# Expert weights, table pieces and block order in the first layers of a transformer kernel: homes for all eight early blocks, a table in six pieces, a single block at the end of both loops

## The chip, the cores and the metric

The kernel runs on one core of a Trainium2 chip. The metric is the device time of one execution in microseconds. All times below are in microseconds. The engines are called by the names that the profile gives them: PE is TensorE (matrix products), DVE is VectorE, ACT is ScalarE, POOL is GpSimd and SP is SyncE, which here only issues DMA transfers. Each engine runs its own queue of instructions in order; semaphores tie the queues together.

## What is computed

The reference is a stack of two macaron blocks on 2048 tokens of width 128 (8 sequences of 256). The part that matters here is the mixture of experts, which is computed twice, before and after an attention:

```python
def _L0_ffn_ref(s, W_in, in_norm_w, Wr, expert_bias, Wg, Wu, Wd, enorm_w, out_norm_w, W_out):
    x = s.reshape(B * T, -1)
    h = rmsnorm(x @ W_in.T, in_norm_w)
    logits = h @ Wr.T
    _, idx = jax.lax.top_k(logits + expert_bias, TOP_K)      # 2 of 8 experts
    sel = jnp.take_along_axis(logits, idx, axis=-1)
    g_topk = jax.nn.softmax(sel, axis=-1)
    gates = jnp.zeros_like(logits).at[jnp.arange(N)[:, None], idx].set(g_topk)
    out = jnp.zeros_like(h)
    for e in range(Wg.shape[0]):
        gate = jax.nn.silu(h @ Wg[e].T)                      # 128 -> 512
        up = h @ Wu[e].T                                     # 128 -> 512
        oe = rmsnorm(gate * up @ Wd[e].T, enorm_w[e])        # 512 -> 128
        out = out + gates[:, e:e + 1] * oe
    s_hat = rmsnorm(out, out_norm_w) @ W_out.T
...
x = x + 0.5 * _L0_ffn_ref(_layernorm(x), ...)     # first layer of experts
x = x + _L0_attn_ref(_layernorm(x), ...)
x = x + 0.5 * _L0_ffn_ref(_layernorm(x), ...)     # second layer of experts
x = x + 0.5 * _L1_ffn_ref(...); x = x + _L1_attn_ref(...); x = x + 0.5 * _L1_ffn_ref(...)
```

## The kernel before

**Blocks of rows.** Each token goes to two experts. The kernel scatters a copy of every token's row into a region of its expert in DRAM (`hs`, line 470), reads the regions back in blocks, computes an expert on a block, and scatters the results to `y` in DRAM (line 769), from where the combination of the two results reads them (line 829). A row is 129 floats, 516 bytes.

There are two kinds of blocks. *Early blocks* (numbers 24 to 31 in tile names, called early block 0 to 7 here, one for each expert) are the first 128 rows of an expert; they can be read before all tokens are dispatched, at places known beforehand. *Table blocks* are the rest: numbers 0 to 14 are *pairs* (256 rows), numbers 15 to 23 are *singles* (128 rows). Which expert and which rows a table block has is found at run time, in a table that VectorE computes from the counts (`table`, line 564, in seven steps: counted, summed, paired, spared, singled, named, bounded). "Named" (lines 634 to 643) writes the tile `tab`: the expert of each block (line 634) and its first row (line 639). "Bounded" (lines 648 to 656) writes `far`, which sends rows beyond an expert's count to nowhere; it is first read when the result rows of table block 0 are addressed.

**The loop.** `work` (line 782) runs over the eight early blocks and then over the table blocks in the order of `TURNS[f]`, where f is the layer (0 or 1); blocks in `MORE` run only where the counts need them. For turn i it issues, in this order:

- gate: 4 products `pg` of the block's turned rows with the gate weights (line 722, in float32 each is two passes, so the profile counts 8), then SiLU on ScalarE (line 731)
- turn_rows of the *next* block: `pht`, a transposition of its rows (line 709), scaled by ScalarE for early blocks (line 712) and by VectorE for table blocks (line 714)
- up: 4 products `pu` (line 722), then the gated product `hg` on VectorE (line 738)
- `pieces[i]`, other work hung into turn i (the steps of the table, later a filter)
- down of the *previous* block: products `py` (line 745), squares on ScalarE (line 762), which also write the sums into column 128 of the result rows, the row product on VectorE (line 763, called so here; it reads `py` and the last columns of the weights), addresses (lines 766 and 767) and the scatter by POOL (line 769, one for each 128 rows). `py` has one bank, so the next down product waits for the row product of this one.
- fetches for block i + 3 on SP's queue: its rows, then its weights (`fetch_rows` and `fetch_weights`). For a table block each of these loads a number from `tab` into a register and then issues a DMA.

The weights of an expert are one piece of 832 KB (gate, up, down and norm, `WALL` columns). The pool tag `w` has four buffers; a load waits until the last reader of its buffer is done, which is the row product. Result rows of table blocks (`yrow`) have two buffers: before the squares of a block may be written, the scatters of the block two before it must have landed.

**Early blocks in the first layer.** `first_experts` (line 903) gives the weights of early blocks 0 to 2 places in the attention's idle tiles (`homes`); those of 3 to 7 take pool buffers, and seven of the eight loads are issued at the start of the kernel (line 910). The eighth, of early block 7, is issued in the loop, by the fetch of turn 4, when early block 3 has given its buffer back; table block 0 then takes the buffer of early block 4. The early blocks' rows are in tile `v0`, their result rows in `v1`; the table's scratch is behind the rows in `v0`. In the second layer (`second_lead`) the weights of early blocks 0 to 5 have such places, only 6 and 7 take pool buffers, and two are free.

**The table in the loop.** `run_experts` (line 891), for both layers:

```python
tab, far, steps = table(f, pc, gp, lead, scratch)
steps[0]()
steps = [*steps[1:5], both(*steps[5:7])]
steps += [lambda: None] * (E - len(steps))
experts(f, tab, far, y2s[f], lead["pool"], steps + pieces, lead)
```

So turns 0 to 3 carry one step each, turn 4 carries named and bounded together, and `pieces` (filter, constants for the attention, the clearing of the attention's tiles by POOL) begin at turn 8.

**After the loop** all engines meet at a branch (line 804); SP's reads of `y` wait until all scatters have landed and POOL has passed this on.

Of the kernel before, what the change touches and what calls it, by code (L numbers as in the profile page):

```python
# [22 lines left out]
E, DFF = 8, 512  # L23
# [9 lines left out]
ROW = D + 1  # L33
# [12 lines left out]
LEAD = 6, 8  # L46
LEADING = list(range(NT, NT + E))
TURNS = (
    [0, 1, 2, 15, 3, 4, 5, 16, 6, 7, 8, 17, 9, 10, 18, 11],
    [0, 1, 2, 15, 3, 4, 5, 6, 16, 7, 8, 9, 17, 10, 11, 12],  # L50
)
MORE = [12, 13, 14, 19, 20, 21, 22, 23], [13, 14, 18, 19, 20, 21, 22, 23]
REGION = NTOK + TT
# [5 lines left out]
WALL = 3 * DFF + D  # L59
# [14 lines left out]
def macaron_kernel(ctx: ExitStack, tc: tile.TileContext, a: dict, out: bass.AP):  # L74
# [110 lines left out]
    def both(*pieces):  # L185
        def run():
            for piece in pieces:
                piece()

        return run  # L190
# [488 lines left out]
    def experts(f, tab, far, y2, mp, pieces, lead):  # L679
# [17 lines left out]
        def fetch_rows(t):  # L697
            n, m = f"f{f}_{t}", blocks(t)
            if t in hst:
                return  # L700
            row = nc.values_load(tab[0:1, 0, t : t + 1], engines=[SP], min_val=1, max_val=HS_ROWS - TT)
            hst[t] = mp.tile([P, 2, ROW], F32, tag="hst", name=f"hst_{n}", bufs=4)[:, 0:m]
            nc.sync.dma_start(hst[t], hss[f][bass.ds(row, m * P), :].rearrange("(s p) c -> p s c", p=P))
# [78 lines left out]
        def work(turns, pieces):  # L782
            n = len(turns)
            for t in turns[:3]:
                fetch_weights(t)
                fetch_rows(t)
            turn_rows(turns[0])
            for i, t in enumerate(turns):
                sg = gate(t)
                if i + 1 < n:  # L790
                    turn_rows(turns[i + 1])
                up(t, sg)
                if i < len(pieces):
                    pieces[i]()
                if i > 0:
                    down(turns[i - 1])
                if i + 3 < n:
                    fetch_rows(turns[i + 3])
                    fetch_weights(turns[i + 3])
            down(turns[-1])  # L800

        work(LEADING + TURNS[f], pieces)
# [88 lines left out]
    def run_experts(f, pc, gp, lead, scratch, pieces):  # L891
        tab, far, steps = table(f, pc, gp, lead, scratch)
        steps[0]()
        steps = [*steps[1:5], both(*steps[5:7])]
        steps += [lambda: None] * (E - len(steps))
        experts(f, tab, far, y2s[f], lead["pool"], steps + pieces, lead)
        return weigh_up(f, gp)

    def wide_rows(t, n, o=0):

        return [t[:, o + i * ROW : o + i * ROW + ROW] for i in range(n)]

    def first_experts(parts, gp, pieces, qks, vs):

        with tc.tile_pool(name="moe0", bufs=2, reuse_waits="tile") as mp:
            homes = {0: qks[1][:, 0:WALL], 1: qks[1][:, WALL : 2 * WALL]}
            homes[2] = qks[0][:, 16 * ROW : 16 * ROW + WALL]
            lead = leading(0, gp, homes, wide_rows(vs[0], E), wide_rows(vs[1], E))
            lead["pool"] = mp
            for e in range(7):  # L910
                lead["weights"](e)
            found = {}

            def counted():
                found["pc"] = counts(0)
                zeros(found["pc"], gp)

            i, m = divmod(LEAD[0], TPC)
            parts[i][-2] = both(parts[i][-2], lead["flagged"])
            rows = parts[i][-1]  # L920
            parts[i][-1] = both(partial(rows, range(m)), lead["read"], partial(rows, range(m, TPC)))
            decays = decay_pieces()
            parts[-1][4] = both(parts[-1][4], decays[0])
            parts[-1][-1] = both(counted, parts[-1][-1])
            stagger(parts, 4)
            gates = run_experts(0, found["pc"], gp, lead, vs[0][:, E * ROW :], pieces)
        return gates, decays[1:]

    def second_lead(gp, qks, vs, ms):
# [658 lines left out]
    with tc.manual_schedule(engines={EN.PE, EN.DVE, EN.Activation, EN.SP}):  # L1588
        with tc.tile_pool(name="rows0", bufs=2) as gp:
            with tc.tile_pool(name="heads", bufs=1, reuse_waits="tile") as hp:  # L1590
                constant_pieces, attention, (*qks, v0, v1, m0, m1) = heads(hp)
                fold_in()
                parts = [[*dispatch(0, i, EARLY, gp)] for i in range(len(EARLY))]
                early = filter_pieces()
                idle = [fold_out, fold_mu, *constant_pieces()]
                idle += [lambda: None] * (len(early) - len(idle))
                pieces = [both(*two) for two in zip(early, idle)]
                gates, decays = first_experts(parts, gp, pieces, qks, (v0, v1))
                mixed = combined(0, gates, y2s[0], gp)
                lead = second_lead(gp, qks, (v0, v1), (m0, m1))  # L1600
                attention(mixed, [dispatch(1, i, LATE, gp) for i in range(len(LATE))], decays, lead)
                gates = second_experts(gp, lead, qks[1][:, 2 * WALL :])
            banks.close()
            tail(gates, y2s[1])
# [137 lines left out]
```

## Time and profile before

| what | us |
|---|---|
| median of 6 runs (lowest, highest) | 591.17 (588.67, 592.87) |
| the profiled execution, its own time | 591.93 |
| its span in the profile | 590.1 |
| TensorE busy in the span | 516.4 (88%) |
| first layer: first gate of the early blocks, first scatter of a table block, last scatter | 41.74, 83.80, 158.91 |
| second layer: the same | 370.22, 408.08, 481.37 |
| loads of weights in the loops, issue to landing, median | 4.7 |

How to read it. The page of the profile gives busy times of each engine and the chain of work that ended last, followed back from the end. The timeline gives instructions in order of time: start, length, engine, line, operation, what it writes and reads, and in brackets how long the engine sat idle before and what released it. The lengths of matrix products are modelled; their starts are measured, and the distance of starts is the better measure. SPq is SP's queue; a line there is the issue of a DMA, not its run. The table of stretches gives, for each from:to, its length, the busy time of PE, weight loads, DVE, ACT and POOL with the number of instructions, the share of the full clock that TensorE was granted, the busy share of the DMA engines and GB/s.

### The profile page before, as it was taken

Reading aid. Unit: us, or ns where it says so; the run is one execution under the profiler, and the core shown is the slowest. Engines: PE = TensorE matmul, PEld = TensorE weight load, DVE = VectorE, ACT = ScalarE, POOL = GpSimd, SP = SyncE. Lnnn points to the kernel's source line nnn. Section 1 sums busy time; section 2 is a strip of 40 time slices with the busy share of each in tenths; the row PEclk is TensorE's granted clock in tenths of the full one; section 3 lists DMA queues with packets and bytes.
Section 4 is the critical chain, followed back from the end, with each engine's and each line's share of the span. In section 5 each row is a group of like instructions: output and inputs, shape, how many; then the busy total and the mean of one; then the engine's idle time right before and its main releaser. Section 6 shows DMA issues by size and latency. Waiting matters only on the chain.

```text
span 590.1 us, 11358 instructions
## 1 busy us (share of the span) xinstructions
PE 516.4 (88%) x3954; PEld 401.8 (68%) x3954; DVE 357.3 (61%) x1129; ACT 277.7 (47%) x683; POOL 194.0 (33%) x202
## 2 busy tenths in 40 slices
PE   5459799999789989998898896989999978789996
PEld 5349798898645555565455553989999945468884
DVE  5776454564335766767767876664344324668775
ACT  4563232223334556557656654433232315884375
POOL 0677445753331201011002356532342335410100
PEclk9559899999989999999999999899999988989999
DMA  8833757666040355064063017455777515000002
GB/s 313 365 91 123 238 196 214 179 203 212 25 109 27 47 141 220 1 181 181 8 126 124 28 33 241 166 173 196 221 219 219 155 35 132 1 1 1 1 0 72
DMA packets 37952, 76.96 MB, mean 130 GB/s; under 512 B 4667, under 2 KB 27106, under 8 KB 36608
## 3 DMA queue, kind: packets, MB, share of 16 engines
q1 hardware_dynamic: 33360, 66.62, 37.0%
q0 software_dynamic: 4528, 9.52, 4.5%
q8 instruction: 35, 0.57, 0.4%
q14 instruction: 29, 0.24, 0.1%
HBM read 55.28 MB, written 21.44 MB: 130 GB/s over the span
## 4 chain that ended last, share of the span: by engine, by line
PE 63%; ACT 11%; DVE 11%; DMA 11%; issue 3%; SPq 1%; POOL 1%; DVEq 0%; ACTq 0%; POOLq 0%
PE pg_f L722 10%; PE pu_f L722 10%; PE py_f L745 8%; PE ps L1127 8%; DMA y<-yrow_f,idx_f 5%; ACT es L1164 4%; PE po L1174 3%; PE pvf L1496 2%; PE pgo L1523 2%; DMA hs<-blank 2%; DMA qk<-heads 2%; PE pin_f L374 1%; PE pm L1110 1%; DVE m L1147 1%; PE pht_f L709 1%
## 5 line engine op out<-in xcount | busy, mean ns | idle before, releaser
L1164 ACT ACTIVATE es<-ps 128x1024 f32<-128x1024 f32 x64 | 65.3, 1021 | 53.0 <-PE ps L1127 31.3
L1147 DVE TENSOR_REDUCE m<-pm 128x4 f32<-128x1024 f32 x64 | 77.4, 1220 | 12.9 <-PE pm L1110 12.8
L1127 PE MATMUL ps<-qa,qk 32*128 32x256 f32 x512 | 73.1, 401 | 11.8 <-ACT es L1164 9.5
L769 POOL DMA_INDIRECT y<-yrow_f,idx_f x57 | 56.1, 983 | 79.9 <-issue 44.0
L470 POOL DMA_INDIRECT hs<-hrow,posi_f x64 | 61.7, 964 | 53.9 <-issue 19.6
L738 DVE TENSOR_TENSOR hg_f<-pu_f,sg_f 128x1024 f32<-128x1024 f32 (+1 forms) x48 | 46.5, 969 | 50.1 <-PE pu_f L722 50.0
L1110 PE MATMUL pm<-qk 32*128 32x256 f32 x512 | 73.8, 400 | 0.9 <-ACT qk L1057 0.6
L762 ACT ACTIVATE ysq_f<-py_f 128x128 f32<-128x128 f32 x73 | 19.7, 274 | 102.2 <-PE py_f L745 90.6
L1127 PEld LDWEIGHTS ps<-qa,qk 32*128 32x128 f32 x512 | 43.5, 184 | 29.7 <-ACT es L1164 22.1
L731 ACT ACTIVATE sg_f<-pg_f 128x1024 f32<-128x1024 f32 (+1 forms) x48 | 39.3, 819 | 45.7 <-PE pg_f L722 45.7
L745 PE MATMUL py_f<-w_f,hg_f 128*128 128x128 f32 x456 | 56.7, 276 | 2.0 <-DVE idx_f L766 1.2
L745 PEld LDWEIGHTS py_f<-w_f,hg_f 128*128 128x128 f32 x456 | 54.9, 192 | 3.6 <-DVE yrow_f L763 2.3
L722 PE MATMUL pg_f<-ht_f,w_f 128*128 128x256 f32 (+1 forms) x256 | 54.8, 357 | 0.1
L722 PE MATMUL pu_f<-ht_f,w_f 128*128 128x256 f32 (+1 forms) x256 | 54.7, 357 | 0.0
L1110 PEld LDWEIGHTS pm<-qk 32*128 32x128 f32 x512 | 44.5, 184 | 3.4 <-issue 1.5
L722 PEld LDWEIGHTS pu_f<-ht_f,w_f 128*128 128x128 f32 x256 | 43.0, 191 | 4.5
L722 PEld LDWEIGHTS pg_f<-ht_f,w_f 128*128 128x128 f32 x256 | 42.9, 191 | 4.3 <-issue 0.3
L171 POOL TENSOR_TENSOR cf_f<-cf_f,mhalf 128x8 f32<-128x8 f32 (+1 forms) x9 | 13.5, 1502 | 65.6 <-DVE cf_f L834 64.2
L763 DVE TENSOR_TENSOR yrow_f<-py_f,w_f 128x256 f32<-128x256 f32 (+1 forms) x32 | 12.7, 396 | 35.7 <-ACT ysq_f L762 33.1
L1174 PE MATMUL po<-es,v 128*32 128x256 f32 x512 | 34.3, 385 | 0.0
L1159 DVE TENSOR_TENSOR qa<-pmt,qk 128x256 f32<-128x256 f32 x32 | 13.5, 422 | 25.7 <-PE pmt L1153 25.6
L714 DVE TENSOR_SCALAR ht_f<-pht_f,pack 128x256 f32<-128x256 f32 (+1 forms) x32 | 14.5, 453 | 17.8 <-PE pht_f L709 17.8
(327 smaller groups left out, 990.0 us busy)
## 6 DMA issues: line engine op xcount, KB each, us to landing
w_f<-in_wall_dram SPq DMA_DIRECT2D x32, 832.0 KB, 4.7
hs<-blank SPq DMA_DIRECT2D x8, 1032.0 KB, 15.7
qk<-in_wall_dram SPq DMA_DIRECT2D x7, 832.0 KB, 5.2
w_lead<-in_wall_dram SPq DMA_DIRECT2D x7, 832.0 KB, 5.7
y_f<-y SPq DMA_DIRECT2D x14, 258.0 KB, 3.4
hst_f<-hs SPq DMA_DIRECT2D x25, 129.0 KB
pack<-in_pack_dram SPq DMA_DIRECT2D x1, 1729.0 KB, 8.6
v<-in_wall_dram SPq DMA_DIRECT2D x2, 832.0 KB
```

What stands on the lines that cost most here:

```text
L470: ins = nc.gpsimd.indirect_dma_start(out=hss[f], out_offset=bass.IndirectOffsetOnAxis(ap=st["posi"][:, t, k : k + 1], axis=0), in_=hrow[:, ...
L722: nc.tensor.matmul(ph[:, k, :], w[t][:, o + k * P : o + k * P + P], ht[t], start=True, stop=True)
L731: nc.scalar.activation(sg, pg, AF.Silu)
L738: nc.vector.tensor_mul(hg[t], pu, sg)
L745: nc.tensor.matmul(py[:, s, :], hg[t][:, k, ts(s, P)], w[t][:, 2 * DFF + k * D : 2 * DFF + k * D + D], start=(k == 0), stop=(k == NFC - 1),)
L762: nc.scalar.activation(sq[:, s], py[:, s], AF.Square, accum_out=yrow[:, s, D : D + 1])
L769: ins = nc.gpsimd.indirect_dma_start(out=y2, out_offset=bass.IndirectOffsetOnAxis(ap=idx[:, s : s + 1], axis=0), in_=yrow[:, s, :], in_off ...
L1110: nc.tensor.matmul(sc[:, jj, i, :], qs[c][r, g, col + i * P : col + (i + 1) * P], ks[c][r, g, col : col + S], start=True, stop=True,)
L1127: nc.tensor.matmul(sc[:, jj, i, :], ks[c][r, g, col + i * P : col + (i + 1) * P], tops[s][r, :], start=True, stop=True,)
L1147: nc.vector.tensor_reduce(m, sc, AX.X, ALU.max, negate=True)
L1164: nc.scalar.activation(es, sc, AF.Exp, scale=scale)
L1174: nc.tensor.matmul(po[32 * j : 32 * j + 32, :], vs[c][:, (b % 2) * 2 + i, (g % 2) * (H // 2) + (g // 2) * 4 + j, :], ess[s, j // 2][:, j % ...
```

## The change

Four edits, in the first layer's early blocks and in the loop that both layers share:

1. The weights of early block 3 get a place in `v1`, so that the pool's four buffers take early blocks 4 to 7, and all eight loads are issued at the start. The early blocks' result rows move from `v1` to `m0` (seven of them) and behind the early rows in `v0` (the eighth). The table's scratch moves from `v0` to `m1`.
2. The table's steps named and bounded are separate pieces: turn 4 carries named, turn 5 carries bounded. This holds for both layers.
3. For the first table block alone (the fetch of turn 5), in both layers, the weights are fetched ahead of the rows on SP's queue.
4. The order of table blocks: in layer 0 single 18 stands behind pair 11, not ahead of it; in layer 1 single 17 stands at the end, behind pair 12, not between pairs 9 and 10. The set of blocks is the same.

```diff
@@ -46,8 +46,8 @@
 TURNS = (
-    [0, 1, 2, 15, 3, 4, 5, 16, 6, 7, 8, 17, 9, 10, 18, 11],
-    [0, 1, 2, 15, 3, 4, 5, 6, 16, 7, 8, 9, 17, 10, 11, 12],
+    [0, 1, 2, 15, 3, 4, 5, 16, 6, 7, 8, 17, 9, 10, 11, 18],
+    [0, 1, 2, 15, 3, 4, 5, 6, 16, 7, 8, 9, 10, 11, 12, 17],
 )
@@ -795,8 +795,10 @@
                 if i + 3 < n:
-                    fetch_rows(turns[i + 3])
-                    fetch_weights(turns[i + 3])
+
+                    first = turns[i + 3] == TURNS[f][0]
+                    for fetch in (fetch_weights, fetch_rows) if first else (fetch_rows, fetch_weights):
+                        fetch(turns[i + 3])
             down(turns[-1])
@@ -891,8 +893,7 @@
         steps[0]()
-        steps = [*steps[1:5], both(*steps[5:7])]
-        steps += [lambda: None] * (E - len(steps))
+        steps = steps[1:] + [lambda: None] * (E + 1 - len(steps))
         experts(f, tab, far, y2s[f], lead["pool"], steps + pieces, lead)
@@ -900,14 +901,15 @@
-    def first_experts(parts, gp, pieces, qks, vs):
+    def first_experts(parts, gp, pieces, qks, vs, ms):
...
-            homes[2] = qks[0][:, 16 * ROW : 16 * ROW + WALL]
-            lead = leading(0, gp, homes, wide_rows(vs[0], E), wide_rows(vs[1], E))
+            homes[2], homes[3] = qks[0][:, 16 * ROW : 16 * ROW + WALL], vs[1][:, 0:WALL]
+            yrows = wide_rows(ms[0], 7) + wide_rows(vs[0], 1, E * ROW)
+            lead = leading(0, gp, homes, wide_rows(vs[0], E), yrows)
             lead["pool"] = mp
-            for e in range(7):
+            for e in range(E):
                 lead["weights"](e)
@@ -923,7 +925,7 @@
-            gates = run_experts(0, found["pc"], gp, lead, vs[0][:, E * ROW :], pieces)
+            gates = run_experts(0, found["pc"], gp, lead, ms[1], pieces)
@@ -1595,7 +1597,7 @@
-                gates, decays = first_experts(parts, gp, pieces, qks, (v0, v1))
+                gates, decays = first_experts(parts, gp, pieces, qks, (v0, v1), (m0, m1))
```

## The prediction

> **What bounds the kernel now.** I read the page first (span, busy shares, chain), then the chain of waits around both expert loops, then the timeline of the engines and of SyncE's queue there, and last the granted clock by stretch.
>
> ```profile
> span 590.1 us, 11358 instructions
> PE 516.4 (88%) x3954; PEld 401.8 (68%) x3954; DVE 357.3 (61%) x1129; ACT 277.7 (47%) x683; POOL 194.0 (33%) x202
> PE 63%; ACT 11%; DVE 11%; DMA 11%; issue 3%; SPq 1%; POOL 1%; DVEq 0%; ACTq 0%; POOLq 0%
> ```
>
> TensorE sets the time, so the change is worth the TensorE idle time that it removes. The chain in the first layer's early blocks (start, length, what):
>
> ```profile
> 59.07 0.28 DVE tab_room L648
> ...
> 60.56 0.23 DVE tab_far L656
> 60.79 0.16 DVE v L763
> ...
> 61.00 5.72 DMA w_lead<-in_wall_dram
> 66.72 0.14 issue
> 66.86 1.45 PE pg_f L722 x8
> ```
>
> The table's last piece runs on VectorE up to 60.79, delays the row product (L763) of early block 3, and only that frees the weight buffer for early block 7, whose load then takes 5.72. The timeline (start, length, engine; in brackets idle time and releaser) shows the stops and the ends of both loops:
>
> ```profile
> 60.99 1.16 PE L745 MATMUL py_f<-w_lead,hg_f 128*128 128x128 f32 x8 [1.53 <-DVE v L763]
> 62.23 0.38 SPq L703 DMA_DIRECT2D hst_f<-hs  x1
> 66.86 1.45 PE L722 MATMUL pg_f<-ht_f,w_lead 128*128 128x128 f32 x8 [1.92 <-DMA w_lead<-in_wall_dram]
> ...
> 153.45 2.05 PE L745 MATMUL py_f<-w_f,hg_f 128*128 128x128 f32 x16 [0.78 <-DVE yrow_f L763]
> 158.91 0.97 POOL L769 DMA_INDIRECT y<-yrow_f,idx_f  x1 [0.31 <-ACT gates L673]
> ...
> 387.81 0.40 SPq L703 DMA_DIRECT2D hst_f<-hs  x1
> 389.00 0.35 SPq L695 DMA_DIRECT2D w_f<-in_wall_dram  x1
> 389.08 1.16 PE L745 MATMUL py_f<-qk,hg_f 128*128 128x128 f32 x8 [1.51 <-DVE m L763]
> ...
> 475.89 2.05 PE L745 MATMUL py_f<-w_f,hg_f 128*128 128x128 f32 x16 [1.18 <-DVE idx_f L766]
> 481.37 0.98 POOL L769 DMA_INDIRECT y<-yrow_f,idx_f  x1 [0.30 <-DVE gates L676]
> ```
>
> Layer one stops twice (1.53 and 1.92), layer two once (1.51). The granted clock by stretch (from:to, length, busy times by engine, clock, DMA share, GB/s) shows what a stop costs afterwards:
>
> ```profile
> 67.50:71.00 3.50, 3.50 (x19) 3.50 (x18) 0.93 (x2) 0.60 (x1) 0.16 (x1) 0.51 1.00 385
> 367.90:371.30 3.40, 2.87 (x12) 2.57 (x13) 2.31 (x14) 1.49 (x2) 2.48 (x4) 0.50 1.00 410
> 371.30:374.70 3.40, 3.40 (x18) 3.40 (x18) 0.38 (x1) 1.02 (x3) 2.49 (x4) 0.50 0.86 335
> ```
>
> After the 1.92 stop TensorE ran at half clock for 3.4 us. At layer two's start the half clock lasted from the first matmul at 368.0 to 374.7, some 6.6 us.
>
> **The change part by part.**
>
> *Early weights and table, layer one.* Warm, eight single-block matmuls take 0.89, a transposition 0.11 (0.21 at half clock). With the table cut in two, the part "named" (57.39 to 59.07) still stands ahead of early block 3's row product, which then ends near 59.3, and block 4's down product starts at 59.33, not 60.99. TensorE goes on without a stop: gate of 6 at 60.25, up of 6 to 62.14, down of 5 at 62.18, gate of 7 at 63.07 (its weights have been there since about 30) to 63.96. The part "bounded" takes 1.72 (59.07 to 60.79). It follows the gated product (0.62) of early block 5 that starts at 59.62, so it runs 60.24 to 61.96, and early block 4's row product frees its weight buffer 0.17 later, at 62.13.
>
> Here the new wait begins. Table block 0 takes that buffer, and SyncE's queue now has its weights ahead of its rows: weights out at 62.17, rows 1.1 later (as 63.95 to 65.07). Today the rows went out at 62.23 and landed at 67.49 by the trace's landing events, 0.77 behind early block 7's weights, hidden under that block's gate. TensorE takes the transposition of these rows before early block 7's up product, so everything from 63.96 on queues behind it, on VectorE too (table block 0's scaling, L714, stands ahead of early block 7's gated product). A weight load took 4.36 (77.15 to 81.51) to 5.72 (61.00 to 66.72); the two nearest are 5.72 and 4.56 (72.47 to 77.03), and I take 5.1. Two-block rows landed 0.36 to 0.90 behind the weights ahead of them; I take 0.75. With 0.14 from landing to TensorE: 62.17 + 5.1 + 0.75 + 0.14 = 68.2 (bounds 67.0 and 68.9). So two stops of 1.53 and 1.92 become one of 4.2. What follows up to table block 0's gate is 2.0 warm (0.22 + 0.89 + 0.89), plus half of a slow spell of 3.4 to 6.6 (I take 5.0): 68.2 + 2.0 + 2.5 = 72.7. Today that gate starts at 71.46. So **+1.2** (bounds: 67.0 + 2.0 + 1.7 = 70.7, -0.7; 68.9 + 2.0 + 3.3 = 74.2, +2.8). The rows of table block 1 and its weights go out behind, at 64.4 and 65.5 (66.45 today), and are needed at about 74 and 77.
>
> [...]
>
> *The same in layer two.* Weight buffers are free there and the rows' copies have their places, so only the order matters. "Named" ends at 387.17; early block 3's row product follows at once, and block 4's down product starts at 387.45 against 389.08: 1.63 gained. In the built program SyncE's two table loads each wait for VectorE on their own, so the weights need only L634 (ends 385.66) and, with the 0.87 from table load to issue, leave at 386.57; the rows leave at about 387.8 as now. Weights land in 4.53 (389.00 to 393.53), rows 0.9 behind (394.43): 392.0, and TensorE can take them at 392.14, when it gets there (393.75 - 1.63 = 392.12). **-1.6**; if the load takes 5.72, only -0.4.
>
> *A single block last.* Rows used: a pair's down product to its first square 1.99 (472.77 to 474.76), to its row product 0.65, on to the next down product 0.48; row product to scatter 1.44, scatter to scatter 1.28; for a single 1.09, 0.40 and 1.30 (151.61, 152.70, 153.10, 154.40). Layer one: the last up product still ends at 151.61; the pair's square is at 153.60, row product 154.25, the single's down product 154.73, scatters 155.69 and 156.97; the single is ready at 157.52, but POOL is busy, so 158.25 against 158.91: **-0.66**. Layer two: before the last up product ends, a pair's down product (1.79) is done in place of the single's (0.89), so 472.77 + 0.89 = 473.66, then 475.65, 476.30, 476.78; scatters 477.74, 479.02, 480.30 against 481.37: **-1.07**. Landing and what follows start from the last scatter, so this reaches the end. Bounds: layer one 0 to -0.7, layer two -0.5 to -1.1.
>
> *The middle of layer two's loop* no longer has a single between blocks 9 and 10; the gate at 463.81 took 1.94 in the chain where others take 1.73, its weights being late: **-0.2** (0 to -0.35).
>
> *Costed at nothing.* The eighth early load at the start: 832 KB; by the packets in the trace each early load moves in 2.0 us and the last ends at 28.1, so 30.2; SyncE next needs it at 34.44, for the twelfth scatter, issued at 31.9. Without that 1.7 of cover each us late would move the early rows. The early blocks' rows in other tiles: the same instructions; POOL's clearing of the first v tile (86.09) now also waits for early block 7's scatter (landed by 83.00): 3 us of cover, and behind it stands only the next scatter.
>
> Sum: +1.2 - 1.6 - 0.66 - 1.07 - 0.2 = **-2.3**. Against the profiled execution's own 591.93 (span 590.1) that is 589.6; it stood 0.76 above the median of the runs, so for the median 591.17 - 2.3 = **588.8**.
>
> **The rivals.** (1) Layer one's rows come early and the clock returns at once: term -0.7, sum -4.2, **587.0**. For: loads of 4.36 to 4.56 in quiet stretches. Against: at 62 to 68 early blocks' scatters share the engines, and the loads there took 5.72 and more. (2) That term at its dear end: +2.8, sum -0.7, **590.4**, no change that can be told. For: the 6.6 spell. (3) Slower: row buffers. Each loop's closing single must wait, before its squares, for the scatters of the pair two blocks back, which has the same of two buffers. Those are issued at 153.40 and 475.45 (as above, one block earlier), and the squares are due at 155.82 and 477.87. POOL's queue leaves 0.73 of slack, so a landing of up to 3.15 is free, and every us beyond costs one at each end. For: beside weight loads a scatter took 5.2 to 5.8 (458.87 to 464.04; 63.63 to 69.46). Against: at the ends no weights move (last issues 140.15 and 461.69), and scatters land in 2.2 to 3.2. At 5.5: -2.3 + 2 x 2.35 = +2.4, **593.6**; it turns slower from a landing of 4.3.
>
> **How the numbers follow.** Under 0.3% (1.8 us) this kernel can't be told from itself. Chances: forecast 0.50, rival one 0.17, two 0.17, three 0.16. The forecast's own range, from its bounds less their corners, is 587.4 to 590.6; about 0.7 of it lies below 589.4. So faster 0.17 + 0.35 = 0.52; same 0.15 + 0.17 = 0.32; slower 0.16. The range takes in rivals one and two and leaves out most of three: 586.8 to 591.8.
>
> **What would show it.** Right: no TensorE wait on early block 7's weights; the stop at 60.99 gone, a wait of 3 to 5 us ahead of the transposition of table block 0's rows with the DMA of hs as releaser, and a half-clock spell behind it; in layer two no stop at 389; last scatters 0.7 and 1.1 sooner against the last up product. Wrong: a table block 0 gate before 70.7 or after 74.2; squares of the closing singles waiting for a scatter; a new stop in layer two over 1 us.

## The result, and the profile after

| | before | after |
|---|---|---|
| median of the runs shown (lowest, highest) | 590.37 of 46 (586.74, 593.42) | 593.78 of 20 (591.30, 596.79) |
| the profiled execution, its own time | 591.93 | 593.28 |
| its span | 590.1 | 591.5 |

The ratio is 1.0065 with a 95% interval of 1.0049 to 1.0081. The change is 3.4 us slower. The forecast was 588.8, 2.3 us faster, with a range of 586.8 to 591.8.

The page of the changed kernel (span, busy time of TensorE, shares of the chain that ended last):

```profile
span 591.5 us, 11348 instructions
...
PE 516.9 (87%) x3954; PEld 401.8 (68%) x3954; DVE 357.6 (60%) x1129; ACT 277.6 (47%) x683; POOL 194.6 (33%) x202
...
PE 44%; ACT 10%; DMA 8%; DVE 7%; issue 2%; POOL 0%; SPq 0%; ACTq 0%; DVEq 0%; POOLq 0%
```

TensorE runs the same 3954 products and is busy 0.5 us longer, so of the 1.4 us between these two spans some 0.9 is idle time. The shares of the chain, 44% here and 63% before, can't be compared: they add up to 71% here, since the chain of the changed kernel is followed back only to 160.14 us, before to 1.45. The timeline of layer one's early blocks (start, length, engine, line, operation; in brackets idle time and releaser):

```profile
61.43 0.33 SPq L695 DMA_DIRECT2D w_f<-in_wall_dram  x1
61.46 1.06 PE L745 MATMUL py_f<-w_lead,hg_f 128*128 128x128 f32 x8
...
63.06 1.63 SPq L703 DMA_DIRECT2D hst_f<-hs  x2
...
67.46 0.69 PE L709 MATMUL pht_f<-ident,hst_f 128*128 128x128 f32 x2 [4.05 <-DMA hst_f<-hs]
...
71.35 2.79 PE L722 MATMUL pg_f<-ht_f,w_f 128*128 128x256 f32 x8
```

Both old stops are gone. One of 4.05 us, for the rows of table block 0, stands in their place. In the table of stretches (from:to, length, busy times of PE, weight loads, DVE, ACT, POOL, then clock, DMA share, GB/s) two spells of half clock of some 6.8 us each show (the expectations call such a spell two windows). One begins 1.2 us before this stop ends, the other stands behind the first loop:

```profile
66.30:73.20 6.90, 5.74 (x23) 5.38 (x24) 1.69 (x5) 0.37 (x2) 0.71 (x1) 0.51 0.63 181
158.50:165.30 6.80, 5.17 (x14) 3.56 (x15) 1.34 (x6) 1.12 (x4) 1.21 (x2) 0.50 0.08 24
```

The timeline at the end of the first loop:

```profile
155.54 1.16 PE L745 MATMUL py_f<-w_f,hg_f 128*128 128x128 f32 x8 [1.18 <-DVE yrow_f L763]
...
159.04 0.97 POOL L769 DMA_INDIRECT y<-yrow_f,idx_f  x1 [0.30 <-DVEq L806]
...
160.13 3.32 PE L197 MATMUL warm_f<-pack,ident 128*128 128x512 f32 x4 [3.43 <-ACT dec L283]
...
163.24 2.94 PE L290 MATMUL ptf<-filt,pack 128*128 128x128 f32 x16
...
164.89 2.99 SPq L831 DMA_DIRECT2D y_f<-y  x6
```

The fetch of y (`y_f`) leaves 5.85 us after the start of the last scatter. Before, these were 158.91 and 163.15, 4.24 apart:

```profile
163.15 2.98 SPq L829 DMA_DIRECT2D y_f<-y  x6
```

And layer two, its early blocks and its end:

```profile
388.70 0.35 SPq L695 DMA_DIRECT2D w_f<-in_wall_dram  x1
...
390.10 1.57 SPq L703 DMA_DIRECT2D hst_f<-hs  x2
...
395.45 0.44 PE L709 MATMUL pht_f<-ident,hst_f 128*128 128x128 f32 x2 [0.86 <-DMA hst_f<-hs]
...
397.52 1.89 PE L722 MATMUL pg_f<-ht_f,w_f 128*128 128x256 f32 x8
...
482.17 0.98 POOL L769 DMA_INDIRECT y<-yrow_f,idx_f  x1 [0.30 <-ACT gates L673]
...
487.00 4.81 SPq L831 DMA_DIRECT2D y_f<-y  x8
```

Here too the stop (1.51) is gone, a smaller one (0.86) has come, and from the last scatter to the fetch of y it is 4.83, before 3.39 (481.37 to 484.76).

The single execution that the profile shows tells of 1.35 us; the medians of 3.4. To see what is typical, the same distances were read from the trace of every kernel below that ran on a chip like this one. For each layer: first gate to the gate of table block 1 (block 1, since a slow spell can run into block 0's gate, as the one to 73.2 does here), from there to the last scatter, from there to the fetch of y.

| kernel | L1 early | L1 loop and tail | L1 landing | L2 early | L2 loop and tail | L2 landing |
|---|---|---|---|---|---|---|
| before | 34.29 | 82.88 | 4.24 | 30.11 | 81.04 | 3.40 |
| after | 35.59 | 82.23 | 5.84 | 29.54 | 80.08 | 4.83 |
| order_l0 | 32.42 | 82.22 | 6.24 | 30.29 | 81.19 | 3.40 |
| order_l1 | 33.53 | 82.88 | 4.25 | 29.74 | 79.45 | 4.93 |
| early_only | 36.29 | 82.91 | 4.24 | 29.25 | 80.53 | 3.65 |
| early_rows_first | 33.05 | 82.89 | 4.40 | 28.39 | 80.50 | 3.41 |
| after_warm | 37.56 | 82.23 | 5.69 | 29.46 | 79.46 | 4.96 |
| four_orders | 31.74 | 82.22 | 6.16 | 28.05 | 79.46 | 4.71 |
| late_branch | 30.90 | 82.22 | 4.82 | 28.71 | 79.44 | 3.69 |
| home_four_2 | 32.87 | 82.87 | 4.24 | 28.92 | 80.97 | 3.39 |

The three kernels with the old early code (before, order_l0, order_l1) have 32.42 to 34.29 in the first column, mean 33.41: the profiled execution of before was the dearest of them. The granted clock goes with this. From the first gate to block 1's it was at half for 8.7 us in before, 2.6 in order_l0 and 4.3 in order_l1 (11.5 in after, 11.6 in early_only). The spell behind the 1.92 stop of before is missing in order_l0, though its stop at the same place is longer (timeline, then stretch; the clock is the third number from the end):

```profile
65.52 1.13 PE L722 MATMUL pg_f<-ht_f,w_lead 128*128 128x128 f32 x8 [2.06 <-DMA w_lead<-in_wall_dram]
65.50:69.00 3.50, 3.13 (x26) 2.96 (x26) 1.17 (x2) 0.91 (x3) 1.17 (x2) 1.00 1.04 381
```

### The profile page after: what moved, and what is told of

It is laid out like the page before. It is cut to its first block, busy times and chain, and to the rows that moved or that the text cites. A ratio compares the mean times of both kernels' runs of the same rounds, so it can differ in the third digit from the quotient of the medians.

```text
span 591.5 us, 11348 instructions
## 1 busy us (share of the span) xinstructions
PE 516.9 (87%) x3954; PEld 401.8 (68%) x3954; DVE 357.6 (60%) x1129; ACT 277.6 (47%) x683; POOL 194.6 (33%) x202
## 4 chain that ended last, share of the span: by engine, by line
PE 44%; ACT 10%; DMA 8%; DVE 7%; issue 2%; POOL 0%; SPq 0%; ACTq 0%; DVEq 0%; POOLq 0%
PE ps L1129 8%; PE pg_f L722 5%; PE pu_f L722 5%; PE py_f L745 4%; ACT es L1166 4%; PE po L1176 3%; DMA qk<-heads 3%; DMA y<-yrow_f,idx_f 3%; PE pvf L1498 2%; PE pgo L1525 2%; PE pm L1112 2%; DVE m L1149 2%; PE pk_m L1442 1%; ACT xn_m L1407 1%; DMA w_f<-in_wall_dram 1%
```

## The experiments

The kernel before was timed beside each group of kernels. It took 590 us on two chips and 620 us on three; a ratio holds for its own chip.

| kernel | before on that chip | this | ratio, 95% interval |
|---|---|---|---|
| order_l0 | 589.70 | 590.56 | 1.0013 (0.9996 to 1.0030) |
| order_l1 | 589.70 | 590.89 | 1.0027 (1.0011 to 1.0044) |
| early_only | 589.70 | 593.05 | 1.0054 (1.0033 to 1.0075) |
| early_rows_first | 589.70 | 587.22 | 0.9944 (0.9919 to 0.9969) |
| after_rows_first | 619.73 | 616.10 | 0.9955 (0.9929 to 0.9980) |
| rows_first_fill | 619.73 | 617.19 | 0.9938 (0.9913 to 0.9962) |
| home_four | 619.73 | 614.43 | 0.9917 (0.9888 to 0.9946) |
| after_warm | 590.36 | 590.84 | 1.0009 (0.9980 to 1.0038) |
| four_orders | 590.36 | 587.57 | 0.9949 (0.9925 to 0.9973) |
| late_branch | 590.36 | 587.99 | 0.9969 (0.9946 to 0.9991) |
| home_four_2 | 590.36 | 587.34 | 0.9963 (0.9937 to 0.9988) |
| home_four_weights | 620.55 | 615.42 | 0.9916 (0.9885 to 0.9946) |
| after_home | 620.55 | 617.52 | 0.9959 (0.9936 to 0.9983) |
| home_four_weights_2 | 620.25 | 615.73 | 0.9931 (0.9906 to 0.9955) |
| after_home_2 | 620.25 | 618.90 | 0.9969 (0.9949 to 0.9989) |
| after_again | 620.87 | 621.87 | 1.0004 (0.9981 to 1.0026) |
| after_home_3 | 620.87 | 616.83 | 0.9926 (0.9897 to 0.9956) |
| home_four_weights_3 | 620.87 | 615.39 | 0.9914 (0.9883 to 0.9945) |

### The parts alone

order_l0 and order_l1 change one row of `TURNS` in the kernel before:

```diff
-    [0, 1, 2, 15, 3, 4, 5, 16, 6, 7, 8, 17, 9, 10, 18, 11],
+    [0, 1, 2, 15, 3, 4, 5, 16, 6, 7, 8, 17, 9, 10, 11, 18],
```

> The kernel before with the first layer's order of the changed kernel alone (single 18 behind pair 11). Theory A (the loss sits in the early blocks, where table block 0's rows leave behind its weights): the order alone gives the forecast's 0.66 us, ratio 0.999. Theory B (a single at the end of the first loop lets TensorE stop around 150 to 160, and the clock is halved in the filter and the warm-up products that stand ahead of the attention): 1.5 to 2.5 us slower, ratio 1.003 to 1.004, with a half-clock spell of 6.8 us at about 158 to 165 in the trace and the transposition of the combined rows behind the warm-up products.

> The kernel before with the second layer's order alone (single 17 last). Theory A and B both: the forecast's 1.07 + 0.2 = 1.3 us faster, ratio 0.998. A third theory (C: the order itself costs, since with pairs 9 and 10 next to one another the loads of weights come due closer together): 0.5 to 1 us slower, ratio 1.001 to 1.002, with longer waits for weights between blocks 8 and 11.

early_only is the changed kernel with both rows put back. early_rows_first takes edit 3 out of that as well:

```diff
-                    first = turns[i + 3] == TURNS[f][0]
-                    for fetch in (fetch_weights, fetch_rows) if first else (fetch_rows, fetch_weights):
-                        fetch(turns[i + 3])
+                    fetch_rows(turns[i + 3])
+                    fetch_weights(turns[i + 3])
```

> The changed kernel with both orders of blocks as before: homes for all early weights, the table in six pieces and weights ahead of rows remain. Theory A: most of the loss of 3.4 us is here, ratio 1.004 to 1.006, with the 4 us wait ahead of the transposition of table block 0's rows and two windows at half clock in layer one. By the trace of the changed kernel alone +1.3 in layer one and -0.6 in layer two make +0.7, ratio 1.001. Theory B: 1.001 or less, since the loss comes from the orders.

> As early_only, but rows ahead of weights for every block, as before. Theory A: table block 0's rows leave at about 60.5 us and land by 63.5, so early block 7's up and down products go on and TensorE stops only once, for 1 to 2 us, for the weights ahead of block 0's gate, at about 67.5 in place of 71.5; layer two gains 1 to 2 us. Together 3 to 5 us faster than the kernel before, ratio 0.992 to 0.995. Theory B: the order of these two loads matters little, since the weights bound the start of table block 0 anyway: ratio 0.999 to 1.001.

Neither theory has it all, though theory A has the early part. That part costs 3.2 us (0.0054 x 590), and taking edit 3 out of it turns that into a gain of 3.3 (0.0056 x 590). So homes and table in six pieces are worth 0.6%, and the order of two loads costs 1.1%. Each new order, which the forecast had faster, came out slower: by 1.6 us in layer two, and by 0.8 in layer one, where the interval still includes no change. order_l0's trace has the spell of half clock behind the loop that theory B named (156.8 to 163.6). order_l1's median fits theory C, but its trace does not: from block 1's gate to the fetch of y it took 84.38 against 84.44 before. That execution was the fastest of its twelve (589.67; the median is 590.89), so what the median shows beyond it is open.

The timeline of early_rows_first, to be read beside that of the changed kernel:

```profile
60.63 0.38 SPq L703 DMA_DIRECT2D hst_f<-hs  x1
...
62.38 0.35 SPq L695 DMA_DIRECT2D w_f<-in_wall_dram  x1
...
63.25 0.44 PE L709 MATMUL pht_f<-ident,hst_f 128*128 128x128 f32 x2 [0.48 <-DMA hst_f<-hs]
...
68.41 3.50 PE L722 MATMUL pg_f<-ht_f,w_f 128*128 128x256 f32 x8 [2.94 <-DMA w_f<-in_wall_dram]
```

The rows leave 2.4 us sooner, the weights only 0.95 later. TensorE goes on with early block 7 and stops 2.94 for the weights, where the changed kernel stopped 4.05 for the rows and had the transposition, early block 7's up product and a down product still to do behind it.

after_rows_first takes edit 3 out of the changed kernel itself:

> The changed kernel with rows ahead of weights for every block, as before; homes, table in six pieces and both new orders remain. If the order of these two loads is the main loss, and the parts add up (0.9944 without the new orders, 1.0013 and 1.0027 for the orders alone), ratio 0.998, some 6 us (0.010) under the changed kernel. If instead the new orders only cost something beside a late start of the loop, ratio 0.993 to 0.995.

0.9955, with an interval that reaches from the one expectation to the edge of the other. It ran on a chip of the 620 us kind, of which more at the end.

### Why weights ahead of rows lose

SyncE's queue, instruction by instruction, has a semaphore wait on VectorE in the changed kernel from 57.54 to 61.31, directly ahead of the issue of table block 0's weights at 61.43. The table had been ready for them at 57.5; what is waited for is early block 4's row product (61.00 to 61.28), which gives the buffer back. The rows stand behind. If that wait is the cause, edit 3 must lose nothing once the buffer is free. home_four gives early block 4's weights a home too (rows first, orders of before); home_four_weights puts the weights first in layer one on top of it; after_home adds the home to the changed kernel as it is:

```diff
+            homes[4] = vs[0][:, 0:WALL]
+            rows = wide_rows(ms[0], 7) + wide_rows(vs[0], 1, WALL)
-            yrows = wide_rows(ms[0], 7) + wide_rows(vs[0], 1, E * ROW)
-            lead = leading(0, gp, homes, wide_rows(vs[0], E), yrows)
+            yrows = wide_rows(ms[1], 7) + wide_rows(vs[0], 1, WALL + ROW)
+            lead = leading(0, gp, homes, rows, yrows)
...
-            gates = run_experts(0, found["pc"], gp, lead, ms[1], pieces)
+            gates = run_experts(0, found["pc"], gp, lead, qks[1][:, 2 * WALL :], pieces)
```

> early_rows_first (the order of blocks of before, rows ahead of weights) with a home for the weights of early block 4 as well (in the first v tile; the early rows move to the first m tile, the result rows to the second, the table's scratch behind the weights in the second qk tile), so that table block 0's load finds a free buffer. If the wait of 2.94 us ahead of block 0's gate stems from that buffer: weights leave 1.4 to 1.8 us sooner, the wait shrinks to 1.0 to 1.5 us, ratio 0.990 to 0.992 (0.9944 without it). If the loads only get in each other's way sooner: ratio 0.994 to 0.996, the wait moving to block 1.

> home_four again, on the chip of the two kernels above, to compare with them: ratio 0.989 to 0.993.

On the chip of the 590 us kind home_four brought no more than early_rows_first (0.9963 against 0.9944, intervals overlapping), and its trace says why: the weights still left at 62.35. They now stood behind the rows, which stood on the queue to 60.69 for the last dispatch scatter (landed at 60.67). So the free buffer was of no use there with the rows first, and the weights first need a free buffer.

> home_four (orders of before) with the weights of table block 0 ahead of its rows in layer one alone. In the changed kernel these weights were ready to leave at 57.5 us and stood 3.8 us on SyncE's queue for the buffer of early block 4, with the rows behind them; in home_four the rows stand on the queue until 60.7 for the last dispatch scatter and the weights leave at 62.4. Theory H (the order is good or bad only by who stands on the queue): with the buffer free the weights leave at about 57.6 and land by 63, the rows leave at 60.7 as before and land by 63.5; no stop over 1 us, no half-clock window, the gate of table block 1 comes 28.5 to 30 us after the first gate (32.9 in home_four, 34.3 before); ratio 0.985 to 0.990. Theory I (the load needs the DMA engines to itself; rows behind it land 4 us late wherever it starts): ratio 0.994 to 0.998.

> The changed kernel as it is, both orders and weights ahead of rows in both layers, with the one further home for early block 4's weights, so that nothing stands on SyncE's queue for a buffer. Theory H: the early loss goes and the early gain comes, 7 to 8 us under the changed kernel in layer one, ratio 0.991 to 0.995. Theory I: ratio 1.002 to 1.007.

> home_four_weights on another chip. On the chip of the last run the kernel before took 620 us, with VectorE and ScalarE standing still for some 12 us at the start of the early blocks, so table block 0's loads were not late there in any order and the two theories were not told apart. Theory H: the gate of table block 1 comes 28.5 to 30 us after the first gate, ratio 0.985 to 0.990; theory I: 33 to 35 us, ratio 0.994 to 0.998.

> after_home on another chip, for the same reason. Theory H: that gate 28.5 to 30 us after the first, ratio 0.989 to 0.995 where the changed kernel has 1.0065. Theory I: 34 to 36 us, ratio 1.002 to 1.007.

> The changed kernel itself, as the measure for after_home on one and the same chip: ratio 1.004 to 1.009 on a chip where the kernel before takes 590 us; on one where it takes 620 us both theories leave it open.

> after_home beside the changed kernel on one chip. Theory H (weights ahead of rows lose only by the buffer wait at the head of SyncE's queue): at least 0.008 under after_again where the kernel before takes 590 us, 0.003 or more where it takes 620. Theory I (weights ahead of rows are bad in themselves): within 0.003 of after_again.

> The best kernel so far on that chip too, with the orders of before: on a chip where the kernel before takes 590 us ratio 0.985 to 0.990 by theory H, 0.994 to 0.998 by theory I; where it takes 620 us 0.990 to 0.994 as in the two runs there.

All of these ran on chips of the 620 us kind, so the numbers expected for the other kind stay untried. after_home's first two ratios (0.9959 and 0.9969) lie between the ranges of both theories. The last three kernels share one chip. The timeline of after_again, which is the changed kernel:

```profile
84.46 0.33 SPq L695 DMA_DIRECT2D w_f<-in_wall_dram  x1
...
86.09 1.55 SPq L703 DMA_DIRECT2D hst_f<-hs  x2
...
89.95 0.44 PE L709 MATMUL pht_f<-ident,hst_f 128*128 128x128 f32 x2 [3.54 <-DMA hst_f<-hs]
...
93.57 1.97 PE L722 MATMUL pg_f<-ht_f,w_f 128*128 128x256 f32 x8
```

and of after_home_3, the same with the further home:

```profile
80.00 0.33 SPq L695 DMA_DIRECT2D w_f<-in_wall_dram  x1
...
81.75 1.56 SPq L703 DMA_DIRECT2D hst_f<-hs  x2
...
86.29 0.44 PE L709 MATMUL pht_f<-ident,hst_f 128*128 128x128 f32 x2 [0.42 <-DMA hst_f<-hs]
...
88.35 1.89 PE L722 MATMUL pg_f<-ht_f,w_f 128*128 128x256 f32 x8
```

The stop goes from 3.54 to 0.42, the gate of table block 0 comes 5.1 us sooner after the first gate (37.12 against 42.20), and the time falls from 621.87 to 616.83, by 5.0: 0.0078 in the ratio, where theory H asked for 0.003 and theory I for less. SyncE's wait for the buffer, 80.48 to 84.34 in after_again, is absent in after_home_3. Rows behind weights are harmless there once the buffer is free, and theory I falls. A gain from weights ahead of rows does not show: on the chip that ran both, home_four_weights (0.9916) lies level with home_four (0.9917).

### The clock behind the stop

after_warm fills the 4 us stop of the changed kernel with products that nobody reads:

```diff
                 if i + 1 < n:
+                    if f == 0 and turns[i + 1] == TURNS[f][0]:
+                        keep_warm(bank("warm_r", "sa"), 16)
                     turn_rows(turns[i + 1])
```

> The changed kernel with 3.7 us of idle products (eight passes, result unused) on TensorE between early block 7's gate and the transposition of table block 0's rows in layer one, so that TensorE works while it waits for these rows. Theory F (half of the early loss is the clock, halved for two windows behind the 4 us stop): no half-clock spell at 66 to 73, the gate of table block 1 comes 33 to 34 us after the first gate in place of 35.6, ratio 1.001 to 1.004 where the changed kernel has 1.0065. Theory G (the rows' landing alone decides): that gate stays at 35 to 36, ratio 1.005 to 1.007.

The median fell to 1.0009, as theory F wants. The profiled execution does not show it:

```profile
62.86 3.60 PE L197 MATMUL warm_r<-pack,ident 128*128 128x512 f32 x8
...
69.73 0.66 PE L709 MATMUL pht_f<-ident,hst_f 128*128 128x128 f32 x2 [3.27 <-DMA hst_f<-hs]
```

In that one the last sixteenth of the rows landed 6.9 us after their issue (62.70 to 69.59; 4.35 in the changed kernel), so TensorE stopped after all and the clock fell to half from 68.7 to 75.5. Eleven of its twelve runs reach from 587.4 to 595.7 (the twelfth took 596.7), more than any other kernel's here. The time speaks for the clock as a large part of the early loss; the trace that would show it is missing.

### Why the single at the end gains nothing

From block 1's gate to the last scatter the single at the end gains what was forecast (82.88 to 82.23 in layer one). But from there to the fetch of y every trace with it in the table takes 1.1 to 2.0 us more, except late_branch's. A scatter lands in sixteen parts. Read from the landing events and the DMA packets marked as instruction fetch (packets of 16,384 bytes), beside TensorE's branch behind the loop and the last scatter's start:

```
layer, kernel       branch   fetch 2 (length)   last scatter   15 parts landed   16th
1 before            154.10   158.60 (1.06)      158.91         161.16            161.20
1 after             156.15   160.56 (1.31)      159.04         161.47            162.94
1 order_l0          153.26   157.88 (1.51)      156.17         158.53            160.45
1 four_orders       152.59   157.17 (1.46)      155.48         157.90            159.69
1 late_branch       153.92   158.48 (1.32)      154.79         157.65            157.67
2 before            476.39   480.67 (1.25)      481.37         483.50            483.50
2 after             479.22   483.75 (0.96)      482.17         484.36            485.74
2 order_l1          475.63   480.02 (1.22)      478.59         480.78            482.26
2 late_branch       477.24   481.70 (1.22)      478.42         480.61            480.85
```

With a single last, one part of sixteen is late, and the rest are not. In these rows a fetch of code starts 4.3 to 4.6 us after TensorE's branch, and its one packet takes 1.0 to 1.5 us. At all twenty loop ends with a single last in the traces here, late_branch's aside, the sixteenth part lands 1.0 to 1.1 us after the end of that packet (160.56 + 1.31 = 161.87, then 162.94); at the eighteen with a pair last it lands 2.1 to 2.5 us after the scatter's start. The trace does not name the DMA engines; that packet and part share one is inferred from these times. With a pair last, branch and last scatter are 4.8 to 5.0 us apart, and this fetch begins ahead of the scatter. With a single last they are 2.9 to 3.0 apart, and the fetch falls 1.4 to 1.7 us into the scatter. Two kernels were to move the branch. rows_first_fill puts idle products behind the last down product:

```diff
             down(turns[-1])
+            if turns[-1] == TURNS[f][-1]:
+                keep_warm(bank(f"warm_x{f}", "sa"), 4)
```

> As after_rows_first, with 0.9 us of idle products (two passes of one 128x512 product, result unused) on TensorE behind the last down product of each loop, ahead of the branch. Theory D (TensorE's second fetch of its code after the branch, 16 KB, starts 4.4 to 4.6 us after the branch and holds one DMA engine 1.0 to 1.5 us, just when the closing single's scatter needs it, 2.9 us after the branch): the fetch then comes behind the scatter's packets, the last scatter lands in 2.2 to 2.5 us in place of 3.6 to 4.3, the fetch of y starts 1.3 to 2 us sooner in each layer, ratio 0.992 to 0.995. Theory E (three scatters close behind one another back up POOL's queue): landing stays at 3.5 to 4.3, ratio as after_rows_first or 0.001 worse.

Its ratio, 0.9938, lies in theory D's range, but it says nothing for theory D: the branch began at 175.78, 0.36 us ahead of the first idle product (176.14), which stands ahead of it in the program: TensorE's sequencer had run ahead of its array. The second fetch hit the scatter as before, and it landed in 3.79 and 3.64. late_branch instead makes TensorE wait for the last row product ahead of the branch, and leaves out the idle products warm_f behind the first branch; four_orders has neither change:

```diff
+            return yrow
...
-            down(turns[-1])
+            last = down(turns[-1])
+            if turns[-1] == TURNS[f][-1]:
+                out = bank(f"held_{f}", "sa")[:, 0:P]
+                nc.tensor.transpose(out, last[:, 0, 0:D], ident)
...
-                keep_warm(bank("warm_f", "pz"), 7)
```

> home_four with both new orders of blocks (a single last). By the forecast's terms for the orders 1.9 us faster than home_four, ratio 0.003 lower. By theory D (the last scatter lands 1.4 to 2 us later in each layer) 0.5 to 2 us slower, ratio 0.001 to 0.003 higher than home_four.

> As four_orders, but TensorE reaches the branch behind each loop later: a transposition of the last block's result rows (result unused) stands ahead of it and waits for VectorE, and the products warm_f behind the first branch are left out. The idle products of rows_first_fill had not moved the branch, since TensorE's sequencer ran ahead of them. Theory D: the branch moves 1.5 to 2 us, the second code fetch starts 0.5 us or more after the last scatter's landing, which takes 2.2 to 2.5 us in place of 3.6 to 4.3; the fetch of y follows 1.2 to 2 us sooner in both layers, ratio 0.001 to 0.004 under four_orders. Theory E (three scatters close behind one another): landing 3.5 to 4.3 as before, ratio as four_orders or higher.

The timelines of four_orders and late_branch at the end of the first loop:

```profile
155.48 0.97 POOL L769 DMA_INDIRECT y<-yrow_f,idx_f  x1 [0.30 <-DVEq L804]
...
156.73 3.33 PE L197 MATMUL warm_f<-pack,ident 128*128 128x512 f32 x4 [3.59 <-ACT dec L283]
...
161.64 2.98 SPq L829 DMA_DIRECT2D y_f<-y  x6
```

```profile
153.31 0.30 PE L804 MATMUL held<-ident,yrow_f 128*128 128x128 f32 x1 [0.88 <-DVE idx_f L766]
...
154.79 0.97 POOL L769 DMA_INDIRECT y<-yrow_f,idx_f  x1 [0.30 <-DVEq L808]
...
157.90 3.75 PE L290 MATMUL ptf<-filt,pack 128*128 128x128 f32 x16 [4.29 <-PEq L808]
...
159.62 2.99 SPq L833 DMA_DIRECT2D y_f<-y  x6
```

With the branch later the second fetch starts 0.8 us behind the landing, the scatter lands in 2.88 and 2.43 in place of 4.21 and 3.46, and the fetch of y follows its start after 4.82 in place of 6.16 (3.69 in place of 4.71 in layer two). Three scatters still follow one another as closely (1.27 us apart), so theory E falls and theory D's account of the landing stands. The time gained nothing, though (0.9969 against 0.9949, intervals overlapping). From the fetch of y to layer two's first gate late_branch takes 210.65 us, four_orders 206.84. The stretches of late_branch and its chain near the end of layer two show what stands there:

```profile
155.90:166.10 10.20, 7.41 (x21) 5.08 (x22) 2.20 (x8) 0.69 (x2) 1.86 (x2) 0.50 0.45 112
476.80:487.00 10.20, 6.19 (x8) 2.71 (x9) 1.38 (x8) 1.39 (x2) 2.12 (x4) 0.50 0.42 106
```

```profile
481.29 10.79 PE warm L197 x18
```

TensorE stands idle 4.29 us ahead of the filter's products, the clock stays at half for 10.2 us at both ends, and in layer two the chain now runs through the warm-up products. Whether the single at the end is worth keeping can't be told: four_orders and home_four_2, which differ in the orders alone, lie at 0.9949 and 0.9963, where theory D had four_orders as the slower.

## Why the prediction was wrong, point by point

**The tail (-0.66 and -1.07, with -0.2 for the middle).** The sizes were right. Layer one gained 0.65 up to the last scatter (82.88 to 82.23). Layer two gained 1.27: the mean of the five traces with the new order is 79.58, that of the five with the old 80.85; forecast 1.07 + 0.2. The step that failed is the next sentence: "Landing and what follows start from the last scatter, so this reaches the end." From there to the fetch of y it takes 5.98 in layer one (mean of the four traces with the single last and the branch in its place) against 4.27, and 4.86 in layer two against 3.45: +1.7 and +1.4. The gains became losses of 1.05 and 0.13. The delay goes on to what follows: from the last scatter of layer one to the first gate of layer two the same four traces take 213.0 to 214.2, those with a pair last 210.8 to 212.0 (early_rows_first 213.8); from the last scatter of layer two to the end of the span it is 109.3 to 110.3 in the four with the single last there, against 107.4 to 108.8. Rival three had the landing of scatters as the danger, but at the squares, for the row buffers; those did not wait (the last square starts at 156.73, right behind its product). Its 593.6 lies beside the measured 593.8 by luck. The prediction's signs of being wrong stop at the squares, so none of them came: block 0's gate is at 71.35 (70.7 to 74.2), the new stop in layer two is 0.86 (1 was the limit). What the delay costs in run time stays open: the orders alone were 0.8 and 1.6 us slower, but four_orders lost nothing against home_four_2.

**Layer one's early blocks (+1.2).** The mechanism was right: one stop of 4.05 (forecast 4.2) in front of the rows' transposition, at 67.46 (68.2), a spell of half clock behind it. The load took 5.22 (forecast 5.1), and the rows landed 0.76 behind it (0.75). Two sizes were off. The spell behind the restart was taken as 5.0 and took 5.7 (67.46 to 73.2): the clock is at half for 6.8 us in the traces of the changed kernel, early_only and after_warm (from 66.3, 66.7 and 68.7). More weighty: the sum was made against one execution, whose early blocks took 34.29, where the same code took 32.42 and 33.53 in two others. The changed code takes 35.59 and 36.29, mean 35.94, against a mean of 33.41: **+2.5**, near the dear end of +2.8 that rival two named. Most of it can be the clock: outside the stops it was at half for 10.3 and 9.4 us in the changed code's two executions and for 5.2 in the mean of the old code's three, and half of the difference, 2.3, is an estimate of what that costs (before, eight single-block products took 1.70 at half clock, from 68.53, and 0.89 at full, from 62.99). So the prediction's reading of what a stop costs, taken from the one spell behind the 1.92 stop, came from the one execution of three that had it.

**Layer two's early blocks (-1.6).** Mean 29.42 (29.54, 29.25, 29.46) against 30.05 (30.11, 30.29, 29.74): **-0.6**. The stop at 389 went as forecast, but the load took 5.29 (388.70 to 393.99), not 4.53, and the rows landed 1.42 behind it, not 0.9. The dear bound, -0.4, was the nearer one. With rows first this stretch takes 28.05 to 28.92 (early_rows_first, four_orders, late_branch, home_four_2), mean 28.52: -1.5.

**Costed at nothing.** The eighth load at the start cost nothing that shows: the first gate is at 41.22 (41.74 before).

**The sum.** +2.5 - 0.6, tails -0.65 + 1.7 and -1.27 + 1.4, make +3.1; the medians show +3.4. The forecast's -2.3 misses these +3.1 by 5.4: 3.1 of it in the two landings, 1.3 in layer one's early blocks, 1.0 in layer two's. That the parts run alone add up to 0.0094 where the whole has 0.0065 lies within their intervals.

**What the prediction didn't ask** is why weights stand ahead of rows at all when their buffer comes free only at 62.13. It wrote both facts down, and costed the order as given. On a chip of the 590 us kind the first two edits without the third and fourth are 0.56% faster than the kernel before (early_rows_first). On the other kind the first two, with the third in layer one and the buffer that it needs, are 0.69 to 0.86% faster (home_four_weights, three chips), and without the third 0.83% (home_four); home_four_weights was never run on the first kind.

## What to carry to other kernels

SyncE's queue ran in order here (3.8 us at its head held the rows behind): before a load is moved to the head of such a queue, ask what it waits for itself. Without a free buffer the new order cost 1.1% of the time (1.0054 against 0.9944); with one it showed neither loss nor gain. A gain at the end of a loop counts from the last landing, not from the last issue, and here a fetch of code behind a branch went along with one late part of that landing (3.90 us after the scatter's start, 2.29 before). And a term of 1 or 2 us read from one execution needs a second one of the same code: here the same early blocks differed by 1.9 us.

## What the runs showed of the hardware

The branch behind each loop, past the code of the `MORE` blocks, is dear for TensorE alone: its compare-and-branch lasts 3.3 to 3.9 us in all twenty traces, and 0.01 to 0.07 us on each of the other four engines. The first product behind it starts 2.4 to 4.0 us after the last one ahead (158.16 after 155.22 before, 160.13 after 156.42 in the changed kernel; 4.5 to 4.6 in late_branch). A fetch of code starts 1.0 to 1.6 us after TensorE's branch (155.10 after 154.10 before), and how much of the 3.3 to 3.9 us is that fetch is not shown. The fetches behind the branch are packets of 16,384 bytes. That these belong to TensorE is inferred from their times, since the trace does not name the engine.

The length of a stop does not by itself decide whether the clock falls. It fell to half behind stops of 1.92 (before) and 2.20 us (home_four_2), and not behind 2.06 (order_l0) and 2.31 (four_orders). Behind the stop of 3.54 in after_again the half clock lasted 3.4 us (90.3 to 93.7), behind that of 4.05 in the changed kernel 6.8.

On the chips of the 620 us kind VectorE stood still for 10.5 to 13.9 us at the start of the first layer's early blocks, with a releaser that the trace calls "remote"; in the ten traces from the others nothing of the kind shows. On one of them the changed kernel was no slower than before (1.0004).
